# Output stores issued two steps after VectorE's last addition, and a different rate of density work in the last 22 steps of an attention-and-density kernel

## The chip, the cores and the metric

The kernel runs on one core of one Trainium2 chip. A core has TensorE (PE, matrix products), VectorE (DVE), ScalarE (ACT), GpSimd (POOL) and SyncE (SP), which here only issues DMA transfers; the engines run their own instruction streams and wait for each other through semaphores. The metric is the device time of one execution in microseconds (us), as the median of several runs.

## The reference

The input x has 8 images of 192 channels and 64 x 64 pixels, all float32. Two layers follow each other, and each adds its result to its input. `_gn` is a group norm of 32 groups (per image, mean and variance over 6 channels and all pixels).

```python
# layer 0, on _gn(x): attention over the 4096 pixels of an image
q = prelu(conv1x1(x, w1, b1), a1)        # 24 channels
k = prelu(conv1x1(x, w2, b2), a2)        # 24 channels
v = prelu(conv1x1(x, wa, ba), aa)        # 192 channels
score = softmax(einsum('bnc,bcm->bnm', q, k), axis=2)
x = x + einsum('bnm,bmc->bnc', score, v)

# layer 1, on _gn(x): a small network per channel, run at x - 0.5 and at x + 0.5
#   for i in range(4): logits = softplus(m[i]) @ logits + b[i]        (1 -> 3 -> 3 -> 3 -> 1)
#                      if i < 3: logits += tanh(f[i]) * tanh(logits)
sign = -sign(lower + upper)
likelihood = abs(sigmoid(sign * upper) - sigmoid(sign * lower))
x = x + maximum(likelihood, 1e-06)
```

## The kernel before

**Steps and blocks.** The attention of an image is cut into 8 blocks (n = 0 to 7) of 512 queries, and a block into 16 steps (`STEPS`), so an image has 128 steps (`IMG`) and the eight images have 1024 (`last`). One step multiplies 256 keys with the block's queries (`scores`, line 802, tile `sc`), takes the exponential on ACT (line 806, tile `e`), and multiplies it with the values (`attend`, line 817, sixteen matmul instructions into tile `b`). The softmax needs a bound per query before the exponential: the same products are made once more, 22 steps (`LEAD`) ahead, into tile `mx` (line 729), reduced by DVE (line 737), and collected at the block's end (line 761). The maxima go to the other layout by two small transfers through DRAM: `nd<-rn` (line 769) two steps after the collection, and four `q<-nd` (line 774) four steps after it. They become one row of the `q` tile, so the first `scores` of a block cannot begin before `q<-nd` has landed. In step numbers within a block of 16, the collection of the *next* block's maxima is at 9, `nd<-rn` at 11, `q<-nd` at 13, and the first `scores` of that block is emitted in step 15. In the last 22 steps there are no maxima left to make.

**A planner writes the order.** All instructions are emitted by one Python loop over steps. `at(t, fn, cost, act, pe)` (line 334) puts a function into the list of step t; `work_off` (line 434) runs, for each step, first that list in the order of its posting (`run_due`), then at most one PE job (`start_job`), then waiting loads (`request`; an `xc` load needs a free buffer, `free["xc"]`, of which there are three), and last `density_step` and one GpSimd piece (`pool_step`). Each engine executes its instructions in the order in which they were emitted. SP's are DMA issues alone: one that waits for a semaphore holds up all that were emitted after it.

**Attention's end.** `finish` (line 828) takes a block's result out of PSUM (`rc`, line 837; `o`, line 841), transposes it (line 850, a PE job) and adds it to the image's pixels in the tile `xc` (line 859), then takes the statistics for the second norm. An image has two `xc` tiles, c = 0 for blocks 0 to 3 and c = 1 for blocks 4 to 7. Each is filled by four DMAs from x (`fetch`, line 1463, issued in `load`, line 109), asked for at steps 6 and 70 of the image. `loaded` is set three steps after the fetch, and the transposes of blocks 0 and 4 are not asked for before. A job may start only in steps 3 to 14 of a block.

**The density.** Layer 1 of image b runs under the attention of image b + 1. Its work is 12 units (`Unit`, line 934: 2 tiles c, 3 channel groups g, 2 signs s), each with 22 additions on DVE (line 1102, 128 x 1024) and 17 activations on ACT (lines 1070 to 1127). `density_step` (line 1243) gives both engines a credit per step: DVE gets `rate`, worked out so that the image's remaining additions end 15 steps into the image after next, with at most `MOST` = 3.3 us, ACT gets 2.9. What other work in the step costs is taken from the same credit. When both signs of a channel group are done, `ending` (line 1295) takes the difference of two tanh, on POOL and ACT up to step `last - 12`, on DVE after it (`alone`: lines 1352, 1364, 1365). Its last function, `store` (line 1376), adds the density to `xc` on DVE (line 1379), issues two stores of 256 KB to the output on SP (line 1382), and, for the last channel group g = 2, sets the `xc` tile free, so that a waiting `xc` load can be issued in the same step.

**The tail.** The last image's density has no attention to run under. After step 1024 `tail_step` (line 1221) gives out work by modelled engine times, in ticks of 1.3 us. The last image's units are made otherwise (`on_pe`): PE forms the sums of the first two layers (line 1041), with 14 DVE operations a unit (11 at line 1102, 3 at line 1060). What is left of image 6 at step 1024 runs in the tail too, ahead of them. The last image's units wait for its second norm, whose chain begins with the reciprocal at line 837.

Of the kernel before, what the change touches and what calls it, by code (L numbers as in the profile page):

```python
# [17 lines left out]
def kernel(  # L18
# [43 lines left out]
    nc = tc.nc  # L62

    B, C, H, W = x.shape
    N = H * W
    CR = w1t.shape[1]
    F = 512
# [4 lines left out]
    R = C // 3  # L72
    STEPS = 16
    IMG = NB * STEPS
    LEAD = STEPS + 6
    ORDER = (0, 2, 1, 3)
    last = B * IMG

    xv = x.rearrange("b (r g) y z -> b r g (y z)", g=3)
    ov = out.rearrange("b (r g) y z -> b r g (y z)", g=3)  # L80
# [37 lines left out]
    for i in range(3):  # L118
        t = xin.tile([128, 3, P], F32, tag=f"xi{i}", name=f"xi{i}")
# [66 lines left out]
    for i in range(2):  # L186
        nc.vector.tensor_reduce(
            out=bb[i], in_=ident[:, 64 * i + CR : 64 * i + 64 : 32], axis=AX.X, op=ALU.add
# [12 lines left out]
    for i in range(2):  # L201
# [3 lines left out]
        for k in range(2):  # L205
            a = a2 if k == i else a1
            nc.scalar.dma_start(
                out=slope[i][64 * k : 64 * k + 64], in_=a.partition_broadcast(64)
# [30 lines left out]
    for src, dst, at, n in (  # L239
# [4 lines left out]
        for s in range(2):  # L244
            nc.sync.dma_start(
                out=dst[R * s : R * s + R, :, at : at + n],
                in_=src.rearrange("(r g) i j -> r g (i j)", g=3),
# [84 lines left out]
    now = [0]  # L332

    def at(t, fn, cost=0.0, act=0.0, pe=0.0):

        due.setdefault(max(t, now[0]), []).append((fn, cost, act, pe))
# [97 lines left out]
    def work_off(t, rate):  # L434
        now[0] = t
        spent.update(DVE=0.0, ACT=0.0)
        for eng in clock:
            clock[eng] = max(clock[eng], (t - last) * TICK)
        run_due(t)
        start_job(t)  # L440
        run_due(t)
        held = set()
        for kind, fn in list(loads):
            if free[kind] > 0 and kind not in held:
                loads.remove((kind, fn))
                fn()
            else:
                held.add(kind)
        density_step(t, rate)
        pool_step()  # L450
# [175 lines left out]
    for i in range(2):  # L626
        t = dram.tile([NC, 64, F], F32, tag=f"qd{i}", name=f"qd{i}")
# [125 lines left out]
    for i in range(2):  # L753
        t = dram.tile([4, 128], F32, tag=f"nd{i}", name=f"nd{i}")
# [34 lines left out]
    xc = {}  # L789
# [96 lines left out]
    OTHER = 0.1  # L886
    MOST = 3.3
    COST = {"DVE": 1.22, "ACT": 1.23, "TANH": 1.05}
# [332 lines left out]
    def tail_step(t):  # L1221

        end = (t - last + 1) * TICK
        more = True
        while more:
            more = False
            for eng in ("PE", "ACT", "DVE"):
                while clock[eng] < end:
                    best = None
                    for n, u in enumerate(list(units)[:4]):  # L1230
                        when = u.ready(eng, list(units)[:n])
                        if when is not None and (best is None or when < best[0]):
                            best = max(when, clock[eng]), u
                            if when <= clock[eng]:
                                break
                    if best is None or best[0] >= end:
                        break
                    best[1].give_out(eng, t, best[0])
                    more = True
                    for u in [u for u in units if not u.busy()]:  # L1240
                        units.remove(u)

    def density_step(t, rate):
        if t >= last:
            return tail_step(t)
        if units:

            left = sum(len(u.todo["DVE"]) for u in units if u.key[0] == units[0].key[0])
            rate = left * COST["DVE"] / max(1, (units[0].key[0] + 2) * IMG + 15 - t) + OTHER
            rate = min(rate, MOST)  # L1250

        for eng, most in (("DVE", rate), ("ACT", ACT_RATE)):
            credit[eng] = min(credit[eng] + most, most + 1.3)
        for eng in ("ACT", "DVE"):
            order = list(range(min(3, len(units))))
            if len(units) == 2:

                order.sort(key=lambda n: -len(units[n].todo["DVE"]))
            for n in order:
                units[n].step(eng, t, list(units)[:n])  # L1260
        for u in [u for u in units if not u.busy()]:
            units.remove(u)
# [17 lines left out]
    def pool_step():  # L1280


        if pieces:
            if len(recent) == 2:
                inst = nc.gpsimd.memset(pause, 0.0)  # L1285
                tc.add_manual_dep(
                    inst.ins, recent[0].ins.name,
                    mybir.DependencyInfo(
                        mybir.DependencyClass.Sync, mybir.DependencyReason.DATA
                    ),  # L1290
                    reason="beside the reduce",
                )
            pieces.popleft()()

    def ending(b, c, g):


        z = [zs.pop((b, c, g, i)) for i in range(2)]
        halves = [slice(h * F, h * F + F) for h in range(2)]
        cell = {}  # L1300

        def later(n, fn, *cost):
            at(now[0] + n, fn, *cost)

        def begin():
            if not bufs:
                later(1, begin)
                return
            endings.pop()
            cell["s"] = bufs.pop(0)  # L1310
            if now[0] < last - 12:
                for h in range(2):
                    pieces.append(lambda h=h: total(h))
            else:
                alone()

        def total(h):
            n = halves[h]
            later(1, lambda: tanhs(h), 0.0, 2.0)
            return nc.gpsimd.tensor_tensor(cell["s"][:, n], z[0][:, n], z[1][:, n], ALU.add)  # L1320

        def tanhs(h):
            for i in range(2):
                nc.scalar.activation(z[i][:, halves[h]], z[i][:, halves[h]], AF.Tanh, scale=0.5)
            s = cell["s"][:, halves[h]]
            nc.scalar.activation(s, s, AF.Sign)
            pieces.append(lambda: difference(h))
            pieces.append(lambda: masked(h))

        def difference(h):  # L1330
            n = halves[h]
            return nc.gpsimd.tensor_tensor(z[0][:, n], z[1][:, n], z[0][:, n], ALU.subtract)  # L1332

        def masked(h):
            n = halves[h]
            if h == 1:
                later(1, lambda: bufs.extend((cell["s"], z[1])))
                later(1, size, 0.0, 1.1)
                later(2, store, 1.3)
            return nc.gpsimd.tensor_tensor(z[0][:, n], z[0][:, n], cell["s"][:, n], ALU.mult)  # L1340

        def alone():

            s = cell["s"]
            parts = halves if (b, c, g) == (B - 1, 1, 2) else [slice(0, 2 * F)]

            def first():

                while pieces:
                    pool_step()  # L1350
                for n in parts:
                    nc.vector.tensor_tensor(s[:, n], z[0][:, n], z[1][:, n], ALU.add)
                later(2, second, 0.0, 2.1)

            def second():
                for n in parts:
                    for i in range(2):
                        nc.scalar.activation(z[i][:, n], z[i][:, n], AF.Tanh, scale=0.5)
                later(2, third, 2.5)

            def third():
                for n in parts:
                    y = z[0][:, n]
                    nc.vector.tensor_tensor(y, z[1][:, n], y, ALU.subtract)
                    nc.vector.scalar_tensor_tensor(y, s[:, n], 0.0, y, ALU.not_equal, ALU.mult)
                bufs.extend((s, z[1]))
                later(2, lambda: size(parts), 0.0, 1.1)
                later(3, lambda: store(parts), 1.3)

            later(1, first, 1.25)  # L1370

        def size(parts=(slice(0, 2 * F),)):
            for n in parts:
                nc.scalar.activation(z[0][:, n], z[0][:, n], AF.Abs, scale=0.5)

        def store(parts=(slice(0, 2 * F),)):
            for n in parts:
                x_ = xc[b, c][:, g, n]
                nc.vector.scalar_tensor_tensor(x_, z[0][:, n], 1e-6, x_, ALU.max, ALU.add)
                for i in range(2):  # L1380
                    k = i * N // 2 + c * 2 * F
                    nc.sync.dma_start(
                        out=ov[b, :, g, k + n.start : k + n.stop], in_=x_[R * i : R * i + R]
                    )
            bufs.append(z[0])
            if g == 2:
                xc.pop((b, c))
                free["xc"] += 1

        endings.append(0)  # L1390
        later(1, begin)
# [132 lines left out]
    for t in range(last):  # L1524
        b = t // IMG
# [21 lines left out]
    t = last  # L1547
# [42 lines left out]
```

## Time and profile before

| what | value |
|---|---|
| median of 3 runs | 4759.76 us (4755.29 to 4764.86) |
| the profiled execution's own time | 4759.02 us |
| its span, first to last instruction | 4757.2 us |
| busy, share of the span | PE 97%, DVE 87%, ACT 68%, POOL 18% |
| attention steps (first to last exponential) | 89.7 to 4409.5 us |
| tail | from 4413 us to 4757 us |
| granted TensorE clock, mean | 0.985 |

In a line of the groups of instructions, `out<-in` names tiles, with the shapes of one instruction behind it, then how many there were, their busy time, the mean of one, and the engine's idle time before them with what ended it. In the views of waits, `A <- B` says that A's engine waited until B was done: total us, number of times, longest. `SPq` is the queue of DMA issues on SP; its waits are the queue's own and not yet anybody else's. In a view of stretches each engine has its busy time with the number of its instructions, then follow the granted TensorE clock (1.00 is full), the share of the DMA engines and GB/s. Matmuls are pipelined, so their busy times overlap, and the distance from start to start tells the pace. The same holds in part for DVE, whose additions of 1.28 us start 1.20 us apart when they stand back to back.

### The profile page before, as it was taken

The page shows a single profiled execution, that of the slowest core. Times are in us where ns is not written, and L with a number is a line of the kernel's source. Part 1 is how long each engine was busy: PE and PEld are TensorE (multiplying, and loading weights), DVE is VectorE, ACT ScalarE, POOL GpSimd, SP SyncE. Part 2 cuts the span into 40 slices and gives each one's busy share as a digit, 9 for nine tenths or more (in the row PEclk, how much of TensorE's full clock was granted, in tenths as well). Part 3 has the DMA queues.
Part 4 walks back from the last instruction along what each step waited for, and adds up shares of the span by engine and source line. Part 5 has one row for each costly group of instructions (what it writes and reads, how often), then busy time and mean ns, then how long its engine had stood idle before and what let it go on. Part 6 is the DMA issues. An engine that isn't in the chain of part 4 may idle for free.

```text
span 4757.2 us, 68763 instructions
## 1 busy us (share of the span) xinstructions
PE 4609.7 (97%) x28116; PEld 3403.4 (72%) x28116; DVE 4125.5 (87%) x4161; ACT 3218.6 (68%) x3687; POOL 869.8 (18%) x841
## 2 busy tenths in 40 slices
PE   8999999999999999999999999999999999999685
PEld 5777777777777777777777777777777777777332
DVE  5433359999999999999999999999999998998898
ACT  2333247777677767877777767777777777778786
POOL 0000001222122212321212312222222222232100
PEclk9999999999999999999999999999999999999797
DMA  2101010111100111110111111111111101001000
GB/s 62 39 19 30 19 45 18 36 24 33 47 22 25 38 40 34 28 34 19 36 47 25 30 41 36 24 29 33 36 36 36 24 23 27 10 6 23 9 14 14
DMA packets 144145, 139.25 MB, mean 29 GB/s; under 512 B 51410, under 2 KB 116948, under 8 KB 143828
## 3 DMA queue, kind: packets, MB, share of 16 engines
q1 hardware_dynamic: 142592, 134.47, 12.1%
q8 instruction: 221, 3.62, 0.4%
q14 instruction: 96, 0.79, 0.1%
q10 hardware_dynamic: 1236, 0.37, 0.0%
HBM read 101.10 MB, written 29.49 MB: 27 GB/s over the span
## 4 chain that ended last, share of the span: by engine, by line
PE 89%; DVE 5%; ACT 3%; DMA 2%; issue 1%; SPq 0%; POOL 0%; ACTq 0%; POOLq 0%; DVEq 0%
PE b L817 57%; PE sc L802 21%; PE b L690 4%; DVE d L1102 3%; PE b L641 2%; PE b L1041 1%; PE mx L729 1%; DMA q<-nd 1%; PE mx_tail L1041 1%; PE b L850 1%; DVE rm L737 1%; DMA out_dram<-xc 0%; ACT d L1095 0%; PE sc_tail L1041 0%; SPq L109 0%
## 5 line engine op out<-in xcount | busy, mean ns | idle before, releaser
L817 PEld LDWEIGHTS b<-v,e 128*128 128x128 f32 x16384 | 2651.8, 190 | 777.8 <-issue 767.2
L817 PE MATMUL b<-v,e 128*128 128x193 f32 x16384 | 2955.6, 334 | 0.0
L806 ACT ACTIVATE e<-sc 128x1024 f32<-128x1024 f32 x1024 | 1044.7, 1020 | 1333.2 <-PE mx L729 1300.1
L737 DVE TENSOR_REDUCE rm<-mx 128x1 f32<-128x1024 f32 x1002 | 1224.1, 1222 | 511.6 <-PE mx L729 499.3
L802 PE MATMUL sc<-q,k 25*128 25x512 f32 x4096 | 1157.7, 641 | 23.6 <-DMA q<-nd 17.6
L729 PE MATMUL mx<-k,q 24*128 24x512 f32 x4008 | 1131.6, 641 | 0.0
L1102 DVE SCALAR_TENSOR_TENSOR d<-d,lc,d 128x1024 f32<-128x1024 f32 x756 | 977.3, 1301 | 17.2 <-ACT d L1079 4.8
L1102 DVE SCALAR_TENSOR_TENSOR d<-d,wsp,d 128x1024 f32<-128x1024 f32 x684 | 877.6, 1285 | 45.3 <-ACT d L1095 36.3
L1285 POOL MEMSET pause<- 128x1 f32 x408 | 40.0, 98 | 3560.9 <-DVE d L1102 3560.9
L1102 DVE SCALAR_TENSOR_TENSOR d<-d,tf,d 128x1024 f32<-128x1024 f32 x540 | 685.2, 1291 | 1.9 <-ACT d L1085 1.8
L1085 ACT ACTIVATE d<-d 128x1024 f32<-128x1024 f32 x540 | 567.2, 1052 | 38.0 <-DVE d L1102 37.7
L802 PEld LDWEIGHTS sc<-q,k 25*128 25x128 f32 x4096 | 308.1, 183 | 253.3 <-issue 205.8
L1095 ACT ACTIVATE d<-d,cb,wsp 128x1024 f32<-128x1024 f32 x348 | 429.9, 1235 | 1.5 <-DVE d L1102 0.6
L1070 ACT ACTIVATE d<-xc,bn,wn 128x1024 f32<-128x1024 f32 x288 | 354.2, 1234 | 0.8 <-issue 0.8
L1133 POOL TENSOR_TENSOR d<-d,d 128x512 f32<-128x512 f32 x168 | 340.9, 2029 | 45.9 <-ACT d L1127 44.8
L1079 ACT ACTIVATE d<-xc,bn,wn 128x1024 f32<-128x1024 f32 x252 | 311.1, 1234 | 0.0
L729 PEld LDWEIGHTS mx<-k,q 24*128 24x128 f32 x4008 | 300.0, 183 | 8.1 <-DVE rm L737 7.5
L1332 POOL TENSOR_TENSOR d<-d,d 128x512 f32<-128x512 f32 x80 | 172.5, 2156 | 0.0
L1320 POOL TENSOR_TENSOR d<-d,d 128x512 f32<-128x512 f32 x80 | 167.2, 2091 | 0.0
L1340 POOL TENSOR_TENSOR d<-d,d 128x512 f32<-128x512 f32 x80 | 159.5, 1994 | 2.0 <-POOL pause L1285 0.3
L690 PE MATMUL b<-wv,xi 64*128 64x192 f32 x1344 | 139.5, 340 | 0.0
L690 PEld LDWEIGHTS b<-wv,xi 64*128 64x128 f32 x1344 | 106.5, 186 | 25.4 <-issue 25.2
(156 smaller groups left out, 2176.9 us busy)
## 6 DMA issues: line engine op xcount, KB each, us to landing
xi<-in_x_dram SPq DMA_DIRECT2D x280, 192.0 KB
xc<-in_x_dram SPq DMA_DIRECT2D x64, 384.0 KB
out_dram<-xc SPq DMA_DIRECT2D x94, 256.0 KB
q<-qd SPq DMA_DIRECT2D x128, 128.0 KB
k<-kq SPq DMA_DIRECT2D x64, 64.0 KB
qd<-kq SPq DMA_DIRECT2D x64, 64.0 KB
q<-nd SPq DMA_DIRECT2D x256, 2.0 KB
d<-in_x_dram SPq DMA_DIRECT2D x16, 192.0 KB
```

Source lines behind the costliest of these rows:

```text
L690: nc.tensor.matmul(pv[:, s, 0:C], lhsT=t[p, g, k * 128 : k * 128 + 128] if g < 3 else one_row[p], rhs=wf["v", b][p, g, :] if g < 3 else wf ...
L729: nc.tensor.matmul(sc[:, s, :], lhsT=tile_of(qt[b, n // 2], n, j)[r], rhs=kt[b][r, u : u + F], start=True, stop=True,)
L737: nc.vector.tensor_reduce(out=rowmax[b, n][:, j, k : k + 1], in_=sc, axis=AX.XY, op=ALU.max)
L802: nc.tensor.matmul(sc[:, s, :], lhsT=kt[b][r, k : k + 128], rhs=qt[b, n // 2][r, :, u : u + 256], start=True, stop=True,)
L806: return lambda: nc.scalar.activation(e, sc, AF.Exp)
L817: nc.tensor.matmul(a[:, j, 0 : C + 1], lhsT=e[:, s, j * 128 : j * 128 + 128], rhs=v[:, s, p % 4, :], start=p == 0 and s == 0 and j % 2 == ...
L1070: nc.scalar.activation(self.buf[k], self.src(), AF.Tanh, bias=bn[:, s, g, 0, i : i + 1], scale=wn[:, g, 0, i : i + 1],)
L1079: nc.scalar.activation(self.buf[k], self.src(), AF.Identity, bias=bn[:, s, g, 1, i : i + 1], scale=wn[:, g, 1, i : i + 1],)
L1085: nc.scalar.activation(self.buf[k], self.buf["l", k[1], k[2]], AF.Tanh)
L1095: nc.scalar.activation(self.buf[k], self.buf["l", n - 1, 0], AF.Identity, bias=offset, scale=wsp[:, g, w : w + 1],)
L1102: nc.vector.scalar_tensor_tensor(dst, src, factor, dst, ALU.mult, ALU.add)
L1133: return nc.gpsimd.tensor_tensor(z[:, n], z[:, n], dst[:, n], ALU.add)
```

## The change

Two things are altered. Up to step 1011, `store` still makes the addition in its step, but the two stores and the release of the `xc` tile go into a new function `send`, which is run two steps later. From step 1012 on the stores stay right behind the addition; a `send` that falls on step 1012 or later no longer gives the tile back to the planner. Second, in the last 22 steps (`t + LEAD >= last`, from step 1002) the rate of density work given to DVE is worked out for an end at step 1032 (`last + 8`) where it was 1039 (image 6: (6 + 2) * 128 + 15), and its upper limit is 4.3 us in place of 3.3.

```diff
@@ density_step
             left = sum(len(u.todo["DVE"]) for u in units if u.key[0] == units[0].key[0])
             rate = left * COST["DVE"] / max(1, (units[0].key[0] + 2) * IMG + 15 - t) + OTHER
             rate = min(rate, MOST)
+            if t + LEAD >= last:
+
+                rate = min(left * COST["DVE"] / (last + 8 - t) + OTHER, MOST + 1.0)
@@ store, in ending
             for n in parts:
                 x_ = xc[b, c][:, g, n]
                 nc.vector.scalar_tensor_tensor(x_, z[0][:, n], 1e-6, x_, ALU.max, ALU.add)
-                for i in range(2):
-                    k = i * N // 2 + c * 2 * F
-                    nc.sync.dma_start(
-                        out=ov[b, :, g, k + n.start : k + n.stop], in_=x_[R * i : R * i + R]
-                    )
+                if now[0] >= last - 12:
+                    send(n)
             bufs.append(z[0])
-            if g == 2:
+            if now[0] < last - 12:
+
+                at(now[0] + 2, send)
+            elif g == 2:
+                xc.pop((b, c))
+
+        def send(n=slice(0, 2 * F)):
+            x_ = xc[b, c][:, g, n]
+            for i in range(2):
+                k = i * N // 2 + c * 2 * F
+                nc.sync.dma_start(
+                    out=ov[b, :, g, k + n.start : k + n.stop], in_=x_[R * i : R * i + R]
+                )
+            if g == 2 and now[0] < last - 12:
                 xc.pop((b, c))
                 free["xc"] += 1
```

## The prediction

> **What bounds the kernel now.** I read the chain that ended last, then who waited for whom on PE inside the loop, then SP's queue around those waits, then stretches of the last steps and of the tail.
>
> ```profile
> PE 89%; DVE 5%; ACT 3%; DMA 2%; issue 1%; SPq 0%; POOL 0%; ACTq 0%; POOLq 0%; DVEq 0%
> PE sc L802 <- DMA q<-nd: 17.6, 7, 5.7
> PE sc L802 <- ACT e L806: 5.7, 6, 2.6
> ```
>
> The loop is PE from end to end. Between 87 and 4412 us PE's own waits name only the two releasers above: 17.6 us in seven waits for the maxima's last transfer, 5.7 us in six for an exponential. Asked window by window, the seven are 5.6 us (image 2, step 32), 5.7 us (image 7, step 32) and 1.2, 1.6, 1.1, 1.1, 1.2 us (step 96 of images 2 to 6). So an SP transfer that PE does not need in the same block costs nothing, and one that delays `q<-nd` costs its full delay.
>
> SP's queue in the timeline around image 7's wait, image 6's second event and image 2's wait (start, us, what, how many):
>
> ```profile
> 4010.45 1.16 SPq L1382 DMA_DIRECT2D out_dram<-xc  x2
> 4014.68 2.56 SPq L109 DMA_DIRECT2D xc<-in_x_dram  x4
> 4017.27 0.60 SPq L769 DMA_DIRECT2D nd<-rn  x1
> 4029.37 2.39 SPq L774 DMA_DIRECT2D q<-nd  x4
> ...
> 4032.65 1.30 PE L802 MATMUL sc<-q,k 25*128 25x512 f32 x2 [5.68 <-DMA q<-nd]
> ...
> 3739.32 0.38 SPq L769 DMA_DIRECT2D nd<-rn  x1
> 3748.01 1.12 SPq L1382 DMA_DIRECT2D out_dram<-xc  x2
> 3751.79 2.56 SPq L109 DMA_DIRECT2D xc<-in_x_dram  x4
> 3754.45 2.38 SPq L774 DMA_DIRECT2D q<-nd  x4
> ...
> 1275.80 0.38 SPq L769 DMA_DIRECT2D nd<-rn  x1
> 1291.10 1.18 SPq L1382 DMA_DIRECT2D out_dram<-xc  x2
> 1294.92 2.56 SPq L109 DMA_DIRECT2D xc<-in_x_dram  x4
> 1297.57 2.38 SPq L774 DMA_DIRECT2D q<-nd  x4
> ```
>
> All waits have one shape: the store of the image's last channel group waits for DVE's addition, the freed tile's load (four DMAs of 384 KB) waits about 3 us for the stores to land, and the maxima's transfer stands behind both: behind the queue, and behind the load's data. In image 7 `nd<-rn` itself is behind the load, and the transfer that reads it is issued 11.5 us later.
>
> ```profile
> 1305.00:1310.00 5.00, 5.00 (x17) 3.50 (x18) 2.81 (x3) 2.81 (x3) 0.00 (x0) 0.50 0.71 190
> 4327.00:4413.00 86.00, 86.00 (x457) 64.96 (x450) 70.18 (x56) 70.64 (x87) 22.18 (x22) 1.00 0.03 7
> 4413.00:4440.00 27.00, 7.57 (x25) 4.80 (x24) 22.67 (x48) 18.75 (x24) 2.20 (x2) 0.62 0.08 20
> 4440.00:4500.00 60.00, 40.50 (x79) 16.30 (x79) 55.01 (x43) 43.62 (x46) 8.82 (x8) 0.80 0.03 9
> ```
>
> Read here the clock of 0.50 after image 2's wait; PE at 86.0 of 86 us in the last 22 steps while DVE has 15.8 us idle; and DVE as the busiest engine after them, 55.0 of 60 us.
>
> **Part 1, the stores.** No instruction is added or removed: 98 stores before and after, each with the same sizes. What changes is SP's order. Its place follows from the transposes of blocks 0 and 4 (line 850): they run in step 30 of images 3 to 6, and `loaded` is three steps after the fetch, so the final addition there is in step 27, behind `nd<-rn` (27, posted earlier) and ahead of `q<-nd` (29). At c = 1 it is step 91 in images 2 to 6, by transposes in step 94. In image 7 they run in step 29, so it is 26; in image 2 they missed step 30 and went to 35, and SP's order leaves 28 for the fetch. Two steps later these become 29, 93, 28 and 30. In steps 29 and 93 `send` is posted two steps before, `q<-nd` four, so `q<-nd` goes first. Term by term:
>
> - Image 2's 5.6 us go: the store comes in step 30, and `q<-nd` follows `nd<-rn` of 1275.8 at once.
> - The five short waits go, 6.2 us: `q<-nd` no longer stands behind the load.
> - Image 7: `nd<-rn` (27) now precedes the store (28), the load still precedes `q<-nd`. In image 6 the load was issued by 3754.35 and PE released at 3761.8, 7.5 us later. The same 7.5 us after 4017.24 is 4024.7; PE was ready at 4032.65 - 5.68 = 4027.0. So the 5.7 us go with 2.3 us to spare. If that spare is gone, up to all of it stays: 0 to 5.7 us, and I take 0.
> - The slow clock after a wait. PE resumed at 1304.8 and was at 0.50 to 1310, which is 5.2 x 0.5 = 2.6 us of lost work; in image 7 from 4032.6 to 4037, 2.2 us; at image 3's 1.6 us wait the stretch 2130 to 2133 has a clock of 0.57, 1.3 us. Together 6.1 us.
> - The tile is freed two steps later, so the load and `loaded` move too. The transposes of block 0 go from step 30 to 35, those of block 4 from 94 to 99 (steps 31 and 95 are too late in their block). They are six matmuls of 0.11 us pace there as here, and need only be done by the image's end. Image 2 already has its pair at 35 and 37: from first to last exponential it took 549.0 us against image 4's 539.8, and after 5.6 + 2.6 us for the wait 1.0 us is left. So 0 to 1.0 us an event, nine events; I take 0, because no PE row differs, and keep 9 as an end.
> - The stores are moved past `xi` loads, `k<-kq` and `qd<-kq` as well. SP waited 894.8 us for line 1379, so what was queued behind those stores starts earlier; PE waits for none of it, so 0. The wait for landed stores before a load (34.5 us, 13 times) stays, now with `xi` loads behind it.
>
> Sum: -(17.6 + 6.1) = -23.7 us, between -15 and -24.
>
> The Trainium skill, "TensorE: Matmul & The Clock Gate", Part 1, says that the clock halves after an idle window of about 3.4 us and comes back after about 3.4 us of sustained work. By it only the two long waits would cost, 1.7 us each as an estimate, 3.4 us in place of 6.1, and the sum would be 4731; the rows disagree on both counts, 5.2 us at 0.50 in image 2 and a halved clock after 1.6 us of idling in image 3, and the rows decide.
>
> **Part 2, the last 22 steps.** On DVE, 50 additions (line 1102) stand between the last collection (line 761) and the last reciprocal (line 837), which is step 1001 to 1023, and of the 164 behind it 12 x 11 = 132 belong to image 7, so 32 of image 6 are left. At step 1002 there were about 80. The rate was 80 x 1.22 / 37 + 0.1 = 2.74 us a step; now it is 80 x 1.22 / 30 + 0.1 = 3.35 us, and the new limit of 4.3 is not reached. What is left shrinks in proportion: 80 x 15 / 37 = 32 before, 80 x 8 / 30 = 21 now. So 11 additions, at a pace of 1.20 us 13.2 us of DVE work, leave the tail. PE's steps give them cover: DVE would be 83.4 us busy in 86. ACT must keep up: 11 x 17 / 22 = 8.5 activations of 1.13 us pace, 9.6 us on 70.6 of 86. If that cover fails, an exponential comes late; the six such waits before cost 5.7 us in the whole loop, and I keep 3 us as the price.
>
> What the tail makes of it: at most -13.2 us, as DVE is its busiest engine until image 6 is done (4493). Against that, 16.6 us of DVE's idle time between 4330 and 4417 was waiting on ACT and will partly remain, so some of the 11 additions will run late, ahead of line 837, and hold up the chain to image 7's norm. Image 7's first DVE operation came at 4465, 26 us after the norm's end, and image 6's additions filled that gap; fewer fill it less. With all 13.2 us late and nothing gained the tail is at 0. I take the middle, -7 us.
>
> **Sum:** 4759.0 (the profiled execution, 0.7 us below the median) - 23.7 - 7 = 4728.3 us.
>
> **Rivals.**
>
> - *The tail gives nothing, or loses.* DVE reaches line 837 late by the 13.2 us, image 7 starts late by as much, and its first PE sums meet the half clock more often: the twelve products of 4443 to 4451.6 took 8.6 us, those of 4453.2 took 5.3. Two such more are +6.6 us. Total 4759.0 - 23.7 + 0 to 7 = 4735 to 4742, say 4739. For it: DVE would have only 2.6 us free in 86. Against: the chain from 4439 to 4490 runs through image 6's additions.
> - *The stores pass nothing that matters.* If the additions sit a step or two earlier than I place them, load and `q<-nd` keep their order and the waits stay. Then only the tail counts: 4752. Against: transposes in step 30 fix the fetch at 27.
> - *Slower: the load lands ahead of the maxima where it did not hurt.* If the later rhythm puts the final addition at step 25 or 26 (89 or 90) in images 3 to 6, two steps more put the load right ahead of `nd<-rn` or `q<-nd`, with image 7's price, 5.7 + 2.2 = 7.9 us. Of the ten such places in images 2 to 6, four make up for the gain; all ten give 4752 + 10 x 7.9 - 12 (waits now there) = 4819. Against: the deadline of 15 steps fixes the end of an image's additions, and five images repeat to the step.
>
> **How the numbers follow.** The forecast 0.58, its own range 4718 to 4735. The tail without gain 0.25. Stores that pass nothing 0.09. Slower 0.08. A measurement here tells 0.2%, 9.5 us. Faster takes the first two, 0.83; same takes the third, 0.09; slower 0.08. The range begins at 4715, which is the full tail (-13.2) with two fewer half-clock groups (-6.6), and goes to 4752, the third case, which also holds the nine transposes' 9 us on the forecast and on the flat tail.
>
> **What would show it.** PE's waits for `q<-nd` gone from the loop, or below 2 us; no clock of 0.5 between 100 and 4400 us; `q<-nd` ahead of the `xc` load in SP's queue at steps 29 and 93; line 850 in steps 35 and 99; about 21 additions of image 6 behind the last line 837, and that line no more than 5 us later behind the last product of line 817; the tail shorter than 344 us by some 7. Wrong would make it: a new wait of PE on `q<-nd` elsewhere, exponentials late in the last 22 steps, or a tail as long as before.

## The result and the profile after

The changed kernel takes 4727.09 us (median of 4 runs, 4725.12 to 4727.45) against 4762.31 us of the kernel before in 4 runs (4755.29 to 4767.1): a ratio of 0.9926 with a 95% interval of 0.9909 to 0.9944, so 0.7% faster. The forecast was 4728 us. The profiled execution after has a span of 4723.3 us, before 4757.2 us, 33.9 us less. Of these, 25.1 us fall before the last exponential (4384.3 us, before 4409.5) and 8.8 us into the tail, which I count from the end of the last product of line 817 to the end of the span (333.7 us, before 342.5). Not all of this is the change's: the first exponential starts 2.0 us later (91.8 us, before 89.7) and image 0, which the change does not touch, is 1.6 us shorter (532.9 us from its first to its last exponential; 534.5 to 535.9 in the eleven other profiles of this study). Images 1 to 7 together take about 25.5 us less: 0, 10.2, 4.2, 2.1, 2.0, 0.9 and 6.2 us, in their order.

PE's own waits in the loop of the changed kernel, asked for 87 to 4400 us; the window reaches past the loop, and the line for L850 belongs to the beginning of the tail:

```profile
PE b L850 <- ACT o L841: 6.4, 1, 6.4
PE sc L802 <- ACT e L806: 5.1, 6, 2.6
PE sc L802 <- DMA q<-nd: 0.9, 1, 0.9
```

The seven waits for the maxima are one of 0.9 us. SP's queue at the two places that were shown of the kernel before, image 7 at steps 27 to 30 and image 6 at steps 91 to 95 (the stores now have line 1396), and PE at what is left of image 7's wait:

```profile
3987.07 0.38 SPq L769 DMA_DIRECT2D nd<-rn  x1
3991.88 1.16 SPq L1396 DMA_DIRECT2D out_dram<-xc  x2
3998.68 2.56 SPq L109 DMA_DIRECT2D xc<-in_x_dram  x4
4001.33 2.38 SPq L774 DMA_DIRECT2D q<-nd  x4
...
4008.61 0.88 PE L802 MATMUL sc<-q,k 25*128 25x512 f32 x2 [0.87 <-DMA q<-nd]
...
3722.21 0.38 SPq L769 DMA_DIRECT2D nd<-rn  x1
3730.46 2.37 SPq L774 DMA_DIRECT2D q<-nd  x4
3732.93 1.16 SPq L1396 DMA_DIRECT2D out_dram<-xc  x2
3736.72 2.56 SPq L109 DMA_DIRECT2D xc<-in_x_dram  x4
```

In image 6 `q<-nd` now goes out before stores and load. In image 7 `nd<-rn` has passed the stores, the load is still ahead of `q<-nd`, and 0.9 us of the 5.7 remain.

The last 22 steps up to the last product, before and after, a stretch of 87.3 us each:

```profile
4327.50:4414.80 87.30, 87.27 (x458) 66.32 (x458) 70.67 (x57) 72.44 (x88) 22.18 (x22) 1.00 0.03 7
```

```profile
4302.40:4389.70 87.30, 87.26 (x458) 66.24 (x457) 79.14 (x64) 78.01 (x93) 25.22 (x24) 1.00 0.03 7
```

PE is as full and as fast as before, and DVE does 8.5 us more in the same time (79.14 against 70.67), ACT 5.6 us more. The tail is shorter by about as much as DVE does more under cover. Its first two stretches, cut at the same distances from the last product as those of before (27 and 60 us):

```profile
4388.00:4415.00 27.00, 8.16 (x25) 4.69 (x23) 24.34 (x50) 17.44 (x24) 0.00 (x0) 0.58 0.08 19
4415.00:4475.00 60.00, 48.60 (x100) 20.86 (x100) 52.26 (x42) 46.29 (x47) 6.33 (x8) 0.85 0.04 9
```

In the second one PE, which here works for image 7 alone, makes 100 products where it made 79. Image 7's first operation on DVE (line 1060) comes 44.5 us behind the last product, before 50.4, and image 6's last ending 67.3 us behind it, before 78.4.

### The profile page after: what moved, and what is told of

Read it like the earlier page. It is cut to its first block, busy times and chain, and to the rows that moved or that the text cites. A ratio compares the mean times of both kernels' runs of the same rounds, so it can differ in the third digit from the quotient of the medians.

```text
span 4723.3 us, 68784 instructions
## 1 busy us (share of the span) xinstructions
PE 4599.5 (97%) x28116; PEld 3396.1 (72%) x28116; DVE 4119.3 (87%) x4161; ACT 3219.8 (68%) x3687; POOL 878.5 (19%) x841
## 4 chain that ended last, share of the span: by engine, by line
PE 92%; DVE 4%; ACT 3%; DMA 1%; issue 1%; SPq 0%; ACTq 0%; POOL 0%; POOLq 0%; DVEq 0%
PE b L817 59%; PE sc L802 22%; PE b L690 4%; DVE d L1102 3%; PE b L641 2%; PE b L1041 1%; PE mx L729 1%; PE b L850 1%; ACT d L1095 1%; PE mx_tail L1041 1%; ACT d L1085 0%; ACT e L806 0%; ACT d L1070 0%; PE sc_head L729 0%; DVE d L1060 0%
## 5 line engine op out<-in xcount | busy, mean ns | idle before, releaser
L1041 PE MATMUL b<-d,v 128*128 128x512 f32 x216 | 106.4, 647 | 30.0 <-ACT b L1025 26.5
```

## The experiments

In the table, "loop" is the time from the first to the last exponential of the profiled execution, "waits" PE's waits on `q<-nd` in it, "left" the additions of image 6 behind the last line 837. The kernel before took 4762 to 4763 us in all these comparisons. The last four columns are of one execution each: for the changed kernel the shortest of its four runs, for rate_only, release_only, full_a and full_da_end4 the longest of theirs. The loop of the changed kernel also has the short image 0, 1.6 to 3.0 us below all others. The six profiles with the old rate in the last 22 steps have tails of 341.4 to 345.1 us, so tails vary by some 4 us.

| kernel | median us (ratio, 95%) | loop us | waits us (count) | left | tail us |
|---|---|---|---|---|---|
| before | 4762.31 | 4319.7 | 17.6 (7) | 32 | 342.5 |
| the changed kernel | 4727.09 (0.9926, 0.9909 to 0.9944) | 4292.5 | 0.9 (1) | 27 | 333.7 |
| stores_only | 4733.88 (0.9942, 0.9930 to 0.9955) | 4293.8 | 0.6 (1) | 32 | 341.4 |
| rate_only | 4751.07 (0.9979, 0.9970 to 0.9988) | 4322.5 | 17.3 (7) | 27 | 333.2 |
| release_only | 4742.58 (0.9958, 0.9943 to 0.9973) | 4300.2 | 3.7 (1) | 32 | 345.1 |
| others_only | 4763.36 (one run) | 4321.0 | 16.7 (7) | 32 | 345.1 |
| delay1 | 4753.08 (0.9981, 0.9972 to 0.9990) | 4311.4 | 8.2 (6) | 32 | 342.6 |
| late_turn | 4772.38 (one run) | 4333.1 | 20.8 (8) | 32 | 341.7 |
| delay3 | 4724.29 (0.9918, 0.9905 to 0.9932) | 4294.1 | 0 | 27 | 332.4 |
| full_a | 4726.77 (0.9920, 0.9906 to 0.9933) | 4299.8 | 0.7 (1) | 23 | 329.1 |
| full_da_end4 | 4737.09 (0.9945, 0.9931 to 0.9959) | 4304.7 | 0.9 (1) | 14 | 333.3 |
| limit40_delay3 | 4726.63 (0.9926, 0.9912 to 0.9939) | 4295.5 | 0 | 25 | 334.1 |

### Each part alone

```diff
# stores_only: the changed kernel, without
-            if t + LEAD >= last:
-                rate = min(left * COST["DVE"] / (last + 8 - t) + OTHER, MOST + 1.0)
# rate_only: the kernel before, with these two lines
```

> Only the first part: stores and tile release two steps later, the rate of the last 22 steps as before. Theory (the two parts add up, the loop's gain is the stores' alone): PE's waits on q<-nd 0.9 us as after the change, the last product of line 817 near 4390 us of the span, 32 additions of image 6 left and a tail of about 342 us; 4734 to 4737 us. Rival (the tail's 8.8 us come from the shifted order in general, not from the rate): a tail near 334 us and 4727 us.

> Only the second part: the new rate in the last 22 steps, stores as before. Theory: waits on q<-nd stay at 17 to 18 us in seven, last product of line 817 near 4415 us, 27 additions left, tail about 334 us; 8 to 9 us faster than before, 0.2%. Rival (the tail's gain hangs on the stores): tail 342 us and the time of before.

The stores alone give 28.2 us (4733.88 against 4762.05), the rate alone 11.0 us (4751.07), which is 39.2 us, and both together 35.2 with an interval of 27 to 43 us: they add up within what the runs can tell. The loop's gain is the stores': the waits are 0.6 us, the tail is 341.4 us, about as before. The tail's gain is the rate's: 333.2 us with all seven waits still in the loop.

### Which part of the store matters

```diff
# release_only: the kernel before; stores at once, the tile is given back two steps later
-            if g == 2:
+            if g == 2 and now[0] < last - 12:
+                at(now[0] + 2, release)
+            elif g == 2:
+                release()
+
+        def release():
                 xc.pop((b, c))
                 free["xc"] += 1
# others_only: the stores of g = 0 and 1 two steps later, those of g = 2 as before
```

> The stores are issued right behind the addition as before, only the freed xc tile is given back two steps later, so that the next load comes later; rate as before. Theory (it is the load's place in front of q<-nd that costs, not the store's own wait for VectorE): waits on q<-nd below 2 us, as with the first part alone, 4734 to 4738 us. Rival (SP standing behind the store's addition is what delays q<-nd): at least the 5.6 us of image 2 stay, where the store waited 15 us, and the time is 4745 to 4755 us.

> Only the stores of channel groups 0 and 1 are issued two steps later; the last group's, which frees the tile, as before; rate as before. Theory (only the store that frees the tile and the load behind it matter): the seven waits of PE on q<-nd as before, 16 to 18 us, and a time within 6 us of before. Rival (SP's standing behind any store's addition delays PE): the waits shrink by 5 us or more.

Moving the stores that free nothing does nothing: 16.7 us of waits in seven, and a time of 4763.36. Moving only the release, and with it the load, takes six of the seven waits, and images 1 to 6 take the same times as with the stores moved (537.2, 538.8, 537.8, 537.7, 537.7, 539.1 us in both). So the load's place in front of the maxima was the cost, as the theory has it. It isn't all of it, and the forecasts of waits below 2 us and of 4734 to 4738 us were missed (4742.58). In image 7 a wait of 3.7 us is left where the whole change leaves 0.6 to 0.9. SP's queue there in release_only:

```profile
3994.84 1.16 SPq L1382 DMA_DIRECT2D out_dram<-xc  x2
3996.04 0.62 SPq L769 DMA_DIRECT2D nd<-rn  x1
4001.63 2.56 SPq L109 DMA_DIRECT2D xc<-in_x_dram  x4
4006.27 2.39 SPq L774 DMA_DIRECT2D q<-nd  x4
```

Here the store, planned in step 26, still holds `nd<-rn` (27) until DVE's addition is done, and everything behind it runs later. Image 7 takes 507.7 us with it, 501.3 with the stores moved too, so the rival's mechanism, SP standing behind the addition, is real at this one place and worth 6.4 us with the slow clock that follows.

### One step of delay, three steps of delay

```diff
-                at(now[0] + 2, send)
+                at(now[0] + 1, send)      # delay1, rate as before
+                at(now[0] + 3, send)      # delay3, with the new rate
```

> Stores and release one step later in place of two, rate as before. Theory, with the final additions in steps 27 and 91 (images 3 to 6), 28 and 91 (image 2), 26 (image 7): the two long waits go, as the load falls behind q<-nd in image 2 (29) and behind nd<-rn in image 7 (27), but the five waits in step 96 stay, since a load in step 92 is still ahead of q<-nd in 93: 6 to 8 us of waits in five or six, 4741 to 4746 us. Rival (what counts is only that SP is no longer held by the addition, by any delay): all seven go, 4734 to 4737 us.

> The changed kernel with three steps of delay instead of two. Theory by step numbers: only image 7's event alters, its release goes from step 28 to 29 and its load falls behind q<-nd, so the 0.9 us of wait left there go; the other places stay; 4725 to 4727 us, the loop 1 us shorter. Rival (a later release delays the next image's pixels): the loop is longer by 2 us or more.

PE's waits in the loop of delay1:

```profile
PE sc L802 <- DMA q<-nd: 8.2, 6, 1.9
PE sc L802 <- ACT e L806: 6.6, 8, 2.6
PE sc L802 <- ACT d L1079: 1.7, 1, 1.7
```

The step numbers hold: both long waits are gone with one step of delay (0.2 us is left in image 7), and the five of step 96 are there (the one of 1.7 us is image 2's, which this view puts down to another releaser, and one of 0.7 us came up in image 5 at step 32). But the time, 4753.08 us, missed the 4741 to 4746 that I expected. The five waits are longer, 1.7 to 1.9 us instead of 1.1 to 1.6. The transposes that had stood in front of them (0.66 us of PE work in step 94) are gone to step 99 with the later `loaded`, and late_turn below, which moves them alone, has these waits 0.5 to 0.8 us longer as well. After three of the five the clock was halved, after one of five in the kernel before. Images 3 to 6 take 541.8, 541.8, 540.7 and 542.9 us where they took 542.0, 539.8, 539.7 and 540.1: they give back 5.6 of the 15.1 us that images 2 and 7 gain.

With three steps the last wait goes too, and the median is 4724.29 us, 2.8 us below the changed kernel's. That is the lowest time of the study, but the intervals overlap, and a difference of 0.06% is not shown. The loop in the table is longer only through image 0 (535.6 us against 532.9); images 1 to 7 take 1.2 us less, as forecast.

### The transposes by themselves

```diff
# late_turn: the kernel before, with
-                loaded[b, c] = now[0] + 3
+                loaded[b, c] = now[0] + 5
```

> The kernel before, in which only `loaded` is set five steps after the fetch instead of three: the transposes of blocks 0 and 4 go to steps 35 and 99 in images 3 to 6 as in the changed kernel, while stores, release and loads stay where they were. Theory (the move of the transposes is free, it explains at most 1 us an image): images 4 to 6 take 539 to 540 us from first to last exponential as before, and the waits on q<-nd stay. Rival (the transposes' place is worth something by itself): 537.7 us with the changed kernel's transposes although the waits are there.

Neither holds as written: the kernel is slower, 4772.38 us. In images 4 and 5, steps 0 to 87, it moves with the changed kernel within 0.6 us in each group of eight steps against the kernel before, and the sum over them is near 0 (-2.5, +1.5, -0.4, +1.9, -0.8, 0.0, +0.2 us in image 4 from step 32): the transposes' place is free, as I took it. The rest are waits. Those of step 96 grew to 1.7 to 2.4 us, with the halved clock after all five. And the rhythm slipped in two images. In image 6 the store was issued at 3479.7 us, 14 us ahead of the end of a wait of 5.9 us at step 32, where the kernel before has such a wait in images 2 and 7 only; in image 2 that wait shrank from 5.6 to 0.8 us. So a place where the load does not hurt can turn into one where it does when the plan shifts by a step.

### More density in the last steps

With the change only five additions more than before are given out, not the eleven of the forecast. The planner has a hard limit on what an engine may be given in one step, `FULL` (4.0 us on DVE, 3.7 on ACT, line 344). In the order written out for the changed kernel, a rate aimed at step 1028 or 1026 instead of 1032 gives the same order, and so does a higher rate for ACT; only with `FULL` raised are more than 55 additions given out. ScalarE's limit alone holds some back: full_a raises nothing else, and 59 are given out.

```diff
# full_a: the changed kernel, with
-                if spent[eng] + cost > FULL[eng]:
+                if spent[eng] + cost > ({'DVE': 4.0, 'ACT': 6.0} if t + LEAD >= last else FULL)[eng]:
# full_da_end4: both at 6.0, ACT's rate 3.6 and (last + 4 - t) in the last 22 steps
# limit40_delay3: ACT at 4.0, three steps of delay
```

> The changed kernel, with the planner's hard limit on ScalarE's work in one step (FULL, 3.7 us) raised to 6 in the last 22 steps. By the order written out, 59 additions instead of 55 then stand before the last reciprocal, and two operations of an ending (lines 1367, 1368) with them: 23 additions of image 6 are left where 27 were. Theory (what VectorE does under the last attention steps comes off the tail one for one): 7.2 us more work on VectorE, 86 of 87 us busy, tail 327 to 329 us where it was 333.7, 4720 to 4722 us. Rival (VectorE and ScalarE have no more room, exponentials and the last reciprocal come late): the last 22 steps longer than 86.4 us or the reciprocal later than 3 us behind the last product, no gain, 4727 us or more.

> The changed kernel with both hard limits at 6 us, ScalarE's rate at 3.6 (2.9) and the end of the rate at step 1028 (1032), all in the last 22 steps alone. By the order written out 68 additions stand before the last reciprocal and 14 are left. Theory one for one: 18 us more than with the change, of which VectorE has room for 8; the rest runs late and holds up the last reciprocal by about 10 us, so the tail is no shorter than with the other run, 326 to 334 us, 4719 to 4727 us. Rival (the tail is bound by the work left, wherever it stands): tail about 316 us, 4710 us.

> The changed kernel with three steps of delay and ScalarE's limit in a step at 4.0 us instead of 3.7 in the last 22 steps; 57 additions before the last reciprocal, 25 left (27). Theory (VectorE's and ScalarE's room in the last steps is nearly used up, 0.3 us a step does not push an exponential out as 2.3 us did): the last 22 steps stay at 86.4 us and the tail is 2.4 us shorter than with the change, 4721 to 4723 us. Rival: the last steps lengthen by as much, 4724 us or more.

In full_a the tail went down as the theory has it, to 329.1 us, 4.6 of the 7.2 us, and the last 22 steps went up, from 86.4 to 92.2 us, as the rival has it, and the median shows no gain. The profiled execution is the longest of its five, though, which go from 4722.2 to 4728.68 us, so the others may lose less there. PE in the timeline of full_a where most of it is lost:

```profile
4344.57 2.07 PE L802 MATMUL sc<-q,k 25*128 25x512 f32 x4 [2.31 <-ACT e L806]
4346.57 5.14 PE L817 MATMUL b<-v,e 128*128 128x193 f32 x16
4351.55 0.82 PE L850 MATMUL b<-ident,o 128*128 128x128 f32 x6
4352.30 1.13 PE L802 MATMUL sc<-q,k 25*128 25x512 f32 x4
4353.35 2.88 PE L817 MATMUL b<-v,e 128*128 128x193 f32 x16
```

One exponential is 2.3 us late, and the step behind it runs at the halved clock (0.50 from 4346.6 to 4351.2 us): the sixteen products take 5.14 us where the next sixteen take 2.88. The last reciprocal comes 4.7 us behind the last product. In full_da_end4 the last 22 steps take 96.9 us, the last reciprocal comes 6.3 us behind the last product (1.4 with the change), and the tail of 333.3 us is no shorter although only 14 additions are left, which refutes the rival that the work left alone decides. The forecast of 4719 to 4727 us was missed (4737.09): it counted the late reciprocal, but not the longer steps. In limit40_delay3 the last 22 steps take 87.8 us and the tail 334.1; it misses its 4721 to 4723 us and ends at 4726.63. Image 7's first operation on DVE (line 1060) even came 4.3 us earlier in that tail than with the change, 40.2 us behind the last product against 44.5, and the lead was lost by the third of image 7's six endings; why, I did not settle.

## Why the prediction was right, and where it was not

**What bounds the kernel.** Right. Every kernel that took the waits on `q<-nd` away, all or some, gained in the loop. The total came within 1.2 us of 4728.3 partly by luck: the median of the kernel before came out at 4762.3 where I began from 4759.0, and the gain at 35.2 us where I had 30.7.

**The stores.** Forecast -23.7 us, measured -25.1 us up to the last exponential in the pair of profiles, -25.5 in images 1 to 7 (-28.2 by stores_only's medians). By its terms:

- Image 2's 5.6 us and the five short waits, 6.2 us, went as worked out from the step numbers, and delay1 and delay3 confirm the numbers: one step moves exactly the two long waits, three steps the last rest.
- Image 7: "with 2.3 us to spare" failed. The 7.5 us from the load's issue to PE's release held (4001.2 to 4008.6, 7.4 us), but the load was issued 3.2 us later than I took, counted from when PE was ready: 2.6 of it because the stores needed 5.6 us to land instead of 3 (3993.04 to 3998.68), the rest because they went out later. So 0.9 us stayed, inside the range of 0 to 5.7. The long landing goes with the order that I had worked out myself, `nd<-rn` in front of the stores, and for which I counted nothing. The stores go out 5.0 us behind `nd<-rn`, which takes 7.1 to 10.3 us to land wherever `q<-nd` waits for it in this trace. In stores_only, delay1, full_a and full_da_end4 it is the same here, and all five pairs took 5.5 to 5.6 us; in release_only, with `nd<-rn` right behind them, they took 5.6 as well (3996.00 to 4001.63). The other pairs that go out right ahead of a load follow `nd<-rn` by 8.5 us or more, and took 2.5 to 3.1 us but for 3.9 and 4.3 in image 7 of delay3 and limit40_delay3. That a transfer under way slows the stores is what this suggests; no run tried it by itself.
- The slow clock, 6.1 us: no stretch at 0.5 is left between 100 and 4390 us. The image times bear out the sizes: image 2 is 10.2 us shorter (5.6 + 2.6 + 1.2 = 9.4 forecast; a wait of 1.1 us for an exponential in step 26 went as well, which I had not counted), image 7 6.2 us (7.9 forecast, less the 0.9 left; 7.4 in delay3, where nothing is left).
- The rule of the Trainium skill, "TensorE: Matmul & The Clock Gate", Part 1, would have put this term at 3.4 us, as an estimate. The traces disagree with it in more places than the prediction had: of fifteen waits of 1.1 to 1.6 us in step 96 (the kernel before, rate_only, others_only) four were followed by the halved clock, of ten waits of 1.7 to 2.4 us there (delay1, late_turn) eight, and of nine waits of 3.7 us and more in step 32 (all of these but delay1, and release_only) all nine.
- The transposes' move at 0: held, by late_turn, against an end of +9 us. Images 3 to 5 even gained about 1 us each beyond their wait and slow clock (4.2, 2.1 and 2.0 us where I had 2.9, 1.1 and 1.1); where that comes from stays open. The move has a side that I did not see: in step 94 the transposes had covered 0.66 us of the wait in step 96. With that wait gone it plays no part, in delay1 and late_turn it does.
- SP's waits behind line 1379, counted as 0: held for the stores that free nothing, as others_only shows (4763.36 us). The waits went from 894.8 us to 726.6. The one place where SP's standing does cost is `nd<-rn` in image 7, by release_only's 6.4 us, and there the forecast had it in the term of image 7.

**The last 22 steps.** Forecast -7 us, measured -8.8. The number is near, the working is not. "What is left shrinks in proportion ... 21 now" failed: 27 are left, since `FULL` caps what a step can be given (ScalarE's 3.7 us among them, as full_a shows), and the rate's proportion is not reached; I had looked at the limit of 4.3 us alone, which is not the one that binds. So 5 additions moved instead of 11, and an ending's first operation with them, 7.2 us of pace and 8.5 us of busy time. What made up for it, by luck, is that I took half of the moved work as lost to lateness, and nothing was lost. The last reciprocal came 1.4 us behind the last product, before 2.6, and in this pair of profiles the tail took the work off one for one: 8.5 us more under cover, 8.8 us less tail, where tails vary by some 4 us. The lateness that I feared does come, but only beyond what the change gives out, in full_a and full_da_end4, and there through exponentials and the halved clock rather than through the reciprocal alone.

**The rivals.** "The tail gives nothing" did not happen here; it is what the further additions of full_da_end4 do (333.3 us with 14 left, 333.7 with 27). "The stores pass nothing that matters" is refuted by the order in SP's queue. The slower rival's mechanism, a load that lands ahead of the maxima where it did not hurt, showed itself once, in late_turn's image 6.

## What to carry to other kernels

On an in-order DMA queue, look at what stands in front of the small transfer that the busiest engine waits for: here 1.5 MB of load that nobody needed for many steps cost more through its place than through its size, and two steps of planning took it away. A wait of the matmul engine should be priced with the slow clock behind it, which made the 7.9 us of waits of image 2 cost 10.2 us. And before counting on a higher rate, look for every limit that the planner has, not for the one next to the line that is altered.

## What I had not expected of the hardware

- A wait of only 1.1 to 1.6 us can be followed by 3.4 us of halved TensorE clock, in four of fifteen cases here; the nine of 3.7 us and more all were, for 6.8 to 10.2 us.
- The kernel before spreads over 12 us in its first four runs (4755.29 to 4767.1; 21 later ones over 6.5), the changed one over 2.3. The profiles of kernels with the short waits differ in how many of them halve the clock, 1.7 us each; that this makes the spread was not shown.
- A pair of stores of 256 KB each that a load waits for lands 2.5 to 3.1 us after its issue in most places, but after 5.5 to 5.6 us in the five traces where it was issued 5.0 us behind `nd<-rn`, a transfer of 2 KB that was still under way.
